# Layer 0's attention in pairs of tiles, its sums made by TensorE with the identity

## The chip, the cores and the metric

The kernel runs on one core of one Trainium2 chip. The metric is the device time of one execution in microseconds (us). The core has five engines that work side by side, each through its own queue in order: TensorE (PE in the profile; PEld is its loading of weights), VectorE (DVE), ScalarE (ACT), GpSimd (POOL) and SyncE (SP), which here only issues transfers. Products leave TensorE into PSUM, in banks of 512 float32 columns on 128 partitions; everything else lies in SBUF.

## The reference

A model of four layers, each a feed-forward half step, an attention step and the same feed-forward half step again, on `x` of shape (4, 1024, 128) in float32. What the change touches is the attention of layer 0. It is not an attention over the sequence: each token looks at its own 16 heads only.

```python
h, hd = 16, 8
Q = (x @ Wq.T).reshape(b, s, h, hd)
K = (x @ Wk.T).reshape(b, s, h, hd)
V = (x @ Wv.T).reshape(b, s, h, hd)
scores = jnp.einsum('bshd,bstd->bsht', Q, K) / math.sqrt(hd)
attn = jax.nn.softmax(scores, axis=-1)
out = jnp.einsum('bsht,bstd->bshd', attn, V).reshape(b, s, dm)
return out @ Wfc.T
```

So for each token there are 16 x 16 scores, each a sum of 8 products, and 16 x 8 outputs, each a sum of 16 products: 2048 products and 2048 again. `x` of this step is normalised (mean and variance over the 128 channels) before it goes in. The feed-forward of layer 0 is a mixture of 8 experts, of which each token uses two: a product of 128 by 512, a GELU, and one of 512 by 128. It runs before and after the attention with the same weights.

## The kernel before

**The stages.** `run` goes through the stages l0, l1_attn, l2 and l3. The residual stays in SBUF, channels on the partitions: `self.X[b]` is 128 x 1024 for each of the four batches. Stage l0 holds both expert passes of layer 0, its attention, and the first feed-forward of layer 1 (`l1_ffn`).

**The lanes.** Within stage l0 `macaron` lines up the work in lanes: one has the experts (`route` where no other lane does it, `experts`, `combine`), one the attentions (`middle0` to `middle3`) and the layer 1 feed-forwards (`last`), and a late one two of the second pass's routes. Each piece is a generator. `lanes` keeps a clock for each lane, always continues the one whose clock is behind, and adds what the generator yields: `yield 2.6` for a block of experts, `yield 11.2` for a tile of attention. A piece may name others that must be finished first: attention of batch b waits for the combination of the first expert pass of b, the second pass's route of batches 0 and 1 for `middle1`. That gives the order in which instructions are written. The framework then places instructions on the queues by its own priorities, so single instructions of both lanes interleave finely.

**An expert block** (`experts`, L424 to L474) is 128 slots of tokens for one expert: a transfer of the block's weights (L455), a gather (L457), a transpose on TensorE (L461), its copy by VectorE (L463), four products, four GELUs on ScalarE (L468), four products back, an addition on VectorE (L441) and a scatter (L442). A pass has 85 blocks: 23 for batch 0, 23 for batch 1 and 39 for batches 2 and 3 together in the first, and 39, 23 and 23 in the second. A float32 product is written once by `mm` (L227) and appears as two instructions on TensorE.

**Attention** (`l0_attn`, from L498) takes a batch in 8 tiles of 128 tokens. First the squares of the centred residual (L509) give the scale of each token (`scales`, L268 and L270). For a tile, `projected` makes queries, keys and values in one product of 384 columns, tokens on the partitions, and ScalarE scales them out of PSUM (L517). `weighed` is on VectorE: all 2048 products of queries and keys (L525), their sum over the 8 dimensions (L527), the maximum (L529), the subtraction (L530), and then ScalarE's exponential (L532). `summed`: the sum of the weights (L537), its reciprocal (L538), the 2048 products of weights and values (L542), their sum over the 16 heads (L544) and the scaling (L545). TensorE turns the tile, so that channels are on the partitions again (L562), ScalarE copies it into one of four columns of `oS` (L563), and after four tiles the product with `wfc` is added to the residual (L569). Tile i + 1 is weighed ahead of the sums of tile i. The weights of V are permuted on the host so that head comes last; those of Q and K are as given.

Of the kernel before, what the change touches and what calls it, by code (L numbers as in the profile page):

```python
# [12 lines left out]
AF = mybir.ActivationFunctionType  # L13
ALU = mybir.AluOpType
AX = mybir.AxisListType

P = 128
B, S, D = 4, 1024, 128
NH, HD = 16, 8
NE, FC = 8, 4  # L20
NT = S // P
# [87 lines left out]
def _col(v):  # L109
    return np.asarray(v).reshape(-1, 1)  # L110


def _moe_pack(w1, w2, b1, b2):

    w2 = w2.reshape(FC, P, NE, D).transpose(1, 2, 0, 3).reshape(P, NE, FC * D)
    b1 = b1.reshape(NE, FC, P).transpose(2, 0, 1)
    return np.concatenate([w1, w2, b1, np.broadcast_to(b2, (P, NE, D))], 2)


def _packs(i):  # L120

    bc = np.broadcast_to

    l0m = [
        ("w", _moe_pack(
            i["L0_ffn_w1"].transpose(2, 0, 1), i["L0_ffn_w2"].transpose(2, 0, 1), i["L0_ffn_b1"], i["L0_ffn_b2"]
        ))
    ]
    l0s = [("rw", i["L0_ffn_router_w"].T)]
    wv = i["L0_attn_Wv"].T.reshape(D, NH, HD).transpose(0, 2, 1).reshape(D, D)  # L130
    l0a = [
        ("wqkv", np.concatenate([i["L0_attn_Wq"].T, i["L0_attn_Wk"].T, wv], 1)),
        ("wfc", i["L0_attn_Wfc"].T),
    ]

    l1f = [
        ("wg", i["L1_ffn_w_gate"].T),
        ("wu", i["L1_ffn_w_up"].T),
        ("wd", i["L1_ffn_w_down"].T.reshape(HIDC, P, D).transpose(1, 0, 2)),
    ]  # L140

    w = i["L1_attn_w_qkv"]
    turned = [2 * d + 1 if d < HD // 2 else 2 * d - HD for d in range(HD)]

    heads = lambda w, order: w.reshape(P, NH, HD)[..., order].reshape(P, D)
    straight = list(range(HD))
    l1a = [
        ("wq", heads(w[:, :D], straight)),
        ("wqt", heads(w[:, :D], turned)),
        ("wk", heads(w[:, D : 2 * D], straight)),  # L150
        ("wkt", heads(w[:, D : 2 * D], turned)),
        ("wv", w[:, 2 * D :]),
        ("wo", i["L1_attn_w_out"]),
        ("bo", _col(i["L1_attn_b_out"])),
    ]

    l2m = [
        ("w", _moe_pack(
            i["L2_ffn_w1"].transpose(1, 0, 2), i["L2_ffn_w2"].transpose(1, 0, 2), i["L2_ffn_b1"], i["L2_ffn_b2"]
        ))  # L160
    ]
    l2s = [("rw", i["L2_ffn_router_w"]), ("rb", bc(i["L2_ffn_router_b"], (P, NE)))]
    l2a = [
        ("wq", i["L2_attn_Wq"].T),
        ("wkv", np.concatenate([i["L2_attn_Wk"].T, i["L2_attn_Wv"].T], 1)),
        ("bq", _col(i["L2_attn_bq"])),
        ("bk", _col(i["L2_attn_bk"])),
        ("bkv", bc(np.concatenate([i["L2_attn_bk"], i["L2_attn_bv"]]), (P, 2 * D))),
        ("gamma", bc(np.asarray(i["L2_attn_gamma"]).reshape(1, 1), (P, 1))),
    ]  # L170

    l3f = [
        ("wr", i["L3_ffn_W_r"].T),
        ("wk", i["L3_ffn_W_k"].T),
        ("wv", i["L3_ffn_W_v"].T),
        ("mur", _col(i["L3_ffn_mu_r"])),
        ("muk", _col(i["L3_ffn_mu_k"])),
    ]
    a = {k[8:]: v for k, v in i.items() if k.startswith("L3_attn_")}
    at = np.arange(P)  # L180
    turn = at % NH * HD + at // 32 + at % 32 // NH * 4
    l3a = [
        ("maa", np.concatenate([_col(a["time_maa_" + x]) for x in "xwkvrg"], 1)),
        ("w1", a["time_maa_w1"]),
        ("w2", a["time_maa_w2"][:4].reshape(P, D)),
        ("w2l", a["time_maa_w2"][4]),
        ("td", _col(a["time_decay"])),
        ("dw1", a["time_decay_w1"]),
        ("dw2", a["time_decay_w2"]),
        ("u", _col(a["time_faaaa"])),  # L190
        ("wr", a["W_r"]),
        ("wk", a["W_k"]),
        ("wv", a["W_v"][:, turn]),
        ("wg", a["W_g"][:, turn]),
        ("wo", a["W_o"][turn]),
        ("lng", _col(a["ln_gamma"][turn])),
        ("lnb", _col(a["ln_beta"][turn])),
    ]
    return {
        **_constants(),  # L200
        "l0m": l0m, "l0s": l0s, "l0a": l0a, "l1f": l1f, "l1a": l1a,
        "l2m": l2m, "l2s": l2s, "l2a": l2a, "l3f": l3f, "l3a": l3a,
    }


class Macaron:
# [291 lines left out]
    def l0_attn(self, ps, wp, m, b):  # L498
        nc = self.nc
        v = nc.vector  # L500
        X = self.X[b]
        scale = 1.0 / math.sqrt(HD)
        bank = lambda shape=(P, HALF): self.t(ps, list(shape), "bank")
        sq = self.t(wp, [P, S], "sq", bufs=1)
        for h in range(2):
            c = slice(h * HALF, (h + 1) * HALF)
            cen = bank()
            self.mm(cen, self.c0["center"], X[:, c])
            nc.scalar.activation(sq[:, c], cen, AF.Square)  # L509
        r = self.scales(ps, wp, sq, "a")  # L510
        yield 4

        def projected(i):
            pq = bank((P, 3 * D))
            self.mm(pq, X[:, i * P : (i + 1) * P], m["wqkvc"])
            qkv = self.t(wp, [P, 3, D], "qkv", bufs=3)
            nc.scalar.mul(qkv.rearrange("p a b -> p (a b)"), pq, r[:, i : i + 1])  # L517
            return qkv

        def weighed(qkv):  # L520
            q = qkv[:, 0, :].rearrange("p (h d) -> p h d", d=HD)
            k = qkv[:, 1, :].rearrange("p (t d) -> p t d", d=HD)
            sh = [P, NH, NH, HD]
            pr = self.t(wp, sh, "prod", bufs=3)
            v.tensor_tensor(pr, q.unsqueeze(2).to_broadcast(sh), k.unsqueeze(1).to_broadcast(sh), ALU.mult)  # L525
            sc = self.t(wp, [P, NH, NH], "sc")
            v.tensor_reduce(sc, pr, AX.X, ALU.add)  # L527
            mx = self.t(wp, [P, NH, 1], "mx")
            v.tensor_reduce(mx, sc, AX.X, ALU.max)  # L529
            v.tensor_tensor(sc, sc, mx.to_broadcast([P, NH, NH]), ALU.subtract)  # L530
            ex = self.t(wp, [P, NH, NH], "ex")
            nc.scalar.activation(ex, sc, AF.Exp, scale=scale)  # L532
            return ex

        def summed(qkv, ex):
            sm = self.t(wp, [P, NH, 1], "sm")
            v.tensor_reduce(sm, ex, AX.X, ALU.add)  # L537
            v.reciprocal(sm, sm)  # L538
            values = qkv[:, 2, :].rearrange("p (d t) -> p d t", d=HD)
            sh = [P, NH, HD, NH]  # L540
            pv = self.t(wp, sh, "prod", bufs=3)
            v.tensor_tensor(pv, ex.unsqueeze(2).to_broadcast(sh), values.unsqueeze(1).to_broadcast(sh), ALU.mult)  # L542
            o = self.t(wp, [P, NH, HD], "o")
            v.tensor_reduce(o, pv, AX.X, ALU.add)  # L544
            v.tensor_tensor(o, o, sm.to_broadcast([P, NH, HD]), ALU.mult)  # L545
            return o.rearrange("p h d -> p (h d)")


        qkvs = [projected(0), projected(1)]
        exs = [weighed(qkvs[0])]  # L550
        yield 6
        for i in range(NT):
            if i + 2 < NT:
                qkvs.append(projected(i + 2))
            if i + 1 < NT:
                exs.append(weighed(qkvs[i + 1]))
            k = i % 4
            if k == 0:
                oS = self.t(wp, [P, HALF], "oS")
            o = summed(qkvs[i], exs[i])  # L560
            oT = bank((P, P))
            nc.tensor.transpose(oT, o, self.c0["ident"])  # L562
            nc.scalar.copy(oS[:, k * P : (k + 1) * P], oT)  # L563
            yield 11.2
            if k == 3:
                y = bank()
                self.mm(y, m["wfc"], oS)
                c = slice((i - 3) * P, (i + 1) * P)
                v.tensor_tensor(X[:, c], X[:, c], y, ALU.add)  # L569


# [713 lines left out]
```

## Time and profile before

| | |
|---|---|
| median of 3 runs | 3297.95 us (3294.87 to 3299.5) |
| the profiled execution's own time | 3388.92 us |
| its span, first to last instruction | 3387.1 us |
| PE busy over the span | 2861.4 us, 84% |
| DVE busy | 1793.1 us, 53% |
| ACT busy | 1614.4 us, 48% |
| POOL busy | 973.6 us, 29% |
| mean granted TensorE clock | 0.888 of full speed |
| layer 0's attention, first to last instruction | about 160 to 711 us of the span |
| start of layer 1's attention | about 949 us |

Times in the prediction are from the profiled execution unless they are said to be of the timed runs. "Busy" is the time in which an engine has an instruction under way; for TensorE the ends of instructions are modelled and lengths of neighbours overlap, so a busy TensorE can still have room, and the distance between the starts of instructions tells more. "Idle before" is the engine's idle time ahead of a group of instructions and what ended it. The clock is the share of full speed that was granted to TensorE.

### The profile page before, as it was taken

The numbers are of one execution on the slowest core, as the hardware profiler recorded it, in microseconds if no ns is written. First come the engines' busy times: TensorE is split into PE (matmuls) and PEld (weight loads), VectorE is DVE, ScalarE is ACT, GpSimd is POOL, SyncE is SP. The second block draws the span as 40 slices with busy tenths as digits, with TensorE's granted clock in tenths as the row PEclk, the third lists the DMA queues.
The fourth block names the chain that finished last, engine by engine and source line by source line (L and its number), as shares of the span: only waits on it lengthen the run. The fifth ranks groups of instructions, "written<-read, shape, count | busy, mean of one in ns | idle before, by whom it ended". The sixth has DMA issues, their size and how long they took to land.

```text
span 3387.1 us, 48419 instructions
## 1 busy us (share of the span) xinstructions
PE 2861.4 (84%) x18126; PEld 1672.3 (49%) x18126; DVE 1793.1 (53%) x3048; ACT 1614.4 (48%) x3546; POOL 973.6 (29%) x972
## 2 busy tenths in 40 slices
PE   6777758778779999999999998987968877688887
PEld 6655547556533333333333335676757856223323
DVE  3387776853136776776776742434454422354353
ACT  4555525567404665665665663454423444322432
POOL 2465506433330000000000000353404444254353
PEclk7888959889879999999999998998978979687888
DMA  5565516544400000000000000475624656000000
GB/s 169 166 186 172 174 45 188 168 123 134 149 13 2 6 6 4 6 6 16 6 6 3 1 1 18 135 218 170 185 71 144 193 166 188 13 0 7 7 0 13
DMA packets 122890, 277.64 MB, mean 82 GB/s; under 512 B 18016, under 2 KB 67296, under 8 KB 122528
## 3 DMA queue, kind: packets, MB, share of 16 engines
q1 hardware_dynamic: 101792, 231.77, 23.1%
q0 software_dynamic: 20864, 42.77, 4.1%
q8 instruction: 144, 2.36, 0.3%
q14 instruction: 90, 0.74, 0.1%
HBM read 238.43 MB, written 31.85 MB: 80 GB/s over the span
## 4 chain that ended last, share of the span: by engine, by line
PE 68%; DVE 13%; POOL 5%; issue 5%; ACT 5%; DMA 4%; another core or an unknown queue 0%; SPq 0%; POOLq 0%; DVEq 0%; ACTq 0%
PE bank L227 37%; PE two L227 16%; PE o L227 8%; PE s L227 4%; DMA c_y<-res 2%; DVE nm L717 2%; POOL z L1078 1%; DMA res<-e_y,g_target 1%; DVE prod L542 1%; ACT e_h L468 1%; DVE sc L527 1%; POOL res L442 1%; DVE prod L525 1%; PE bank L461 1%; PE wave L227 1%
## 5 line engine op out<-in xcount | busy, mean ns | idle before, releaser
L717 DVE TENSOR_REDUCE nm<-two 128x2 f32<-128x1024 f32 x512 | 626.8, 1224 | 289.2 <-PE s L227 269.8
L740 ACT ACTIVATE e<-s 128x512 f32<-128x512 f32 x1024 | 555.8, 595 | 403.5 <-PE s L227 400.5
L468 ACT ACTIVATE e_h<-bank,e_w 128x128 f32<-128x128 f32 x1304 | 453.3, 367 | 544.2 <-PE bank L227 445.6
L227 PE MATMUL bank<-e_x,e_w 128*128 128x128 f32 x2608 | 573.0, 318 | 152.4 <-ACT e_h L468 61.5
L227 PE MATMUL s<-qm,kz 32*128 32x512 f32 x2048 | 633.5, 642 | 0.8 <-ACT e L740 0.8
L227 PE MATMUL two<-kz,qz 32*128 32x512 f32 x2048 | 592.1, 663 | 19.5 <-DVE nm L717 2.5
L457 POOL DMA_INDIRECT e_xg<-rows,g_source x326 | 328.5, 1008 | 942.1 <-DVE g_target L412 347.5
L227 PEld LDWEIGHTS bank<-e_x,e_w 128*128 128x128 f32 x2608 | 413.8, 203 | 290.4 <-ACT e_h L468 124.3
L442 POOL DMA_INDIRECT res<-e_y,g_target x326 | 376.1, 1154 | 319.5 <-DVE e_y L441 179.9
L227 PE MATMUL bank<-e_w,e_h 128*128 128x128 f32 x2608 | 450.7, 289 | 15.7 <-ACT e_h L468 12.9
L227 PEld LDWEIGHTS bank<-e_w,e_h 128*128 128x128 f32 x2608 | 378.4, 202 | 29.5 <-ACT e_h L468 22.3
L227 PE MATMUL o<-e,va 128*32 128x256 f32 x4096 | 328.3, 392 | 0.1
L441 DVE TENSOR_TENSOR e_y<-bank,e_w 128x128 f32<-128x128 f32 x326 | 94.4, 290 | 438.3 <-PE bank L227 379.5
L227 PEld LDWEIGHTS two<-kz,qz 32*128 32x128 f32 x2048 | 159.3, 188 | 237.5 <-issue 161.0
L227 PEld LDWEIGHTS o<-e,va 128*32 128x32 f32 x4096 | 81.0, 108 | 389.6 <-issue 370.3
L227 PEld LDWEIGHTS s<-qm,kz 32*128 32x128 f32 x2048 | 206.5, 183 | 11.4 <-issue 7.7
L705 POOL COPY va<-vd 128x256 f32<-128x256 f32 x16 | 6.7, 432 | 624.4 <-PE o L227 538.1
L463 DVE COPY e_x<-bank 128x128 f32<-128x128 f32 x326 | 92.8, 285 | 93.6 <-PE bank L461 73.2
L493 PE MATMUL bank<-c,c_y 128*128 128x128 f32 x128 | 39.5, 453 | 111.8 <-DVE c_y L490 111.8
L227 PE MATMUL bank<-g_cols,g_lanes 128*128 128x39 f32 (+1 forms) x512 | 83.3, 321 | 25.5 <-DVE g_cols L392 24.8
L1078 POOL TENSOR_TENSOR z<-st,r 128x512 f32<-128x512 f32 x64 | 96.0, 1503 | 22.7 <-DVE st L1072 22.4
L461 PE MATMUL bank<-c,e_xg 128*128 128x128 f32 x326 | 94.5, 290 | 7.6 <-DMA e_xg<-rows,g_source 7.6
(302 smaller groups left out, 3778.1 us busy)
## 6 DMA issues: line engine op xcount, KB each, us to landing
e_w<-in_l0m_dram SPq DMA_DIRECT2D x170, 578.0 KB
e_w<-in_l2m_dram SPq DMA_DIRECT2D x156, 578.0 KB
c_y<-res SPq DMA_DIRECT2D x32, 512.0 KB
rows<-g_xt SPq DMA_DIRECT2D x16, 512.0 KB
e_xg<-rows,g_source POOLq DMA_INDIRECT x326
res<-e_y,g_target POOLq DMA_INDIRECT x326
x<-in_x_dram SPq DMA_DIRECT2D x4, 512.0 KB
qz<-qd SPq DMA_DIRECT2D x64, 32.0 KB
```

The lines of the kernel that those rows point to most:

```text
L227: self.nc.tensor.matmul(out, lhsT, rhs, start=start, stop=stop)
L441: nc.vector.tensor_tensor(y, o, w[:, MOE_W - D :], ALU.add)
L442: ins = nc.gpsimd.indirect_dma_start(out=res[:, :], out_offset=at(target[:, k : k + 1]), in_=y, in_offset=None)
L457: nc.gpsimd.indirect_dma_start(out=xg, out_offset=None, in_=rows[:, :], in_offset=at(source[:, k : k + 1]))
L461: nc.tensor.transpose(tp, xg, self.c0["ident"])
L463: nc.vector.tensor_copy(x, tp)
L468: nc.scalar.activation(h[:, fc, :], up[:, fc, :], func, bias=w[:, 2 * FC * P + fc : 2 * FC * P + fc + 1])
L493: nc.tensor.transpose(tp[:, j, :], y[1][:, i, :], self.c0["ident"])
L525: v.tensor_tensor(pr, q.unsqueeze(2).to_broadcast(sh), k.unsqueeze(1).to_broadcast(sh), ALU.mult)
L717: v.tensor_reduce(nm[:, it, h, 2 * pair : 2 * pair + 2], s, AX.X, ALU.max, negate=True)
L740: nc.scalar.activation(es[g], s, AF.Exp, scale=scale)
L1078: pool.tensor_tensor(z, st[:, 0:HALF], r, ALU.mult)
```

## The change

Attention takes two tiles at a time. Queries and keys are now permuted on the host so that the dimension of a head comes first and the head last; values are no longer permuted. VectorE still makes all the products, but the sums over them are made by TensorE: the products of a pair lie in 8 planes, one for each dimension, of 2 x 256 numbers, and 8 products of the identity with a plane add up in one PSUM bank, which then holds the scores of both tiles. The maximum and the subtraction read that bank. The weights are scaled before they meet the values; the products of weights and values lie in 16 planes of 128 x 128, one for each head summed over, and 16 products with such a plane as the stationary side and the identity as the moving one add up in PSUM. These come out turned, channels on the partitions, so that the transpose is gone; one copy serves both tiles. The buffers for qkv grow from 3 to 6, those for the first products are one of both tiles instead of three of one, and the second products have two of their own. The pieces that `lanes` counts are 5 and 8 for a pair instead of 11.2 for each tile.

```diff
-    wv = i["L0_attn_Wv"].T.reshape(D, NH, HD).transpose(0, 2, 1).reshape(D, D)
+    inner = lambda w: w.T.reshape(D, NH, HD).transpose(0, 2, 1).reshape(D, D)
     l0a = [
-        ("wqkv", np.concatenate([i["L0_attn_Wq"].T, i["L0_attn_Wk"].T, wv], 1)),
+        ("wqkv", np.concatenate([inner(i["L0_attn_Wq"]), inner(i["L0_attn_Wk"]), i["L0_attn_Wv"].T], 1)),
...
-            qkv = self.t(wp, [P, 3, D], "qkv", bufs=3)
+            qkv = self.t(wp, [P, 3, D], "qkv", bufs=6)
...
-        def weighed(qkv):
-            q = qkv[:, 0, :].rearrange("p (h d) -> p h d", d=HD)
-            k = qkv[:, 1, :].rearrange("p (t d) -> p t d", d=HD)
-            sh = [P, NH, NH, HD]
-            pr = self.t(wp, sh, "prod", bufs=3)
-            v.tensor_tensor(pr, q.unsqueeze(2).to_broadcast(sh), k.unsqueeze(1).to_broadcast(sh), ALU.mult)
-            sc = self.t(wp, [P, NH, NH], "sc")
-            v.tensor_reduce(sc, pr, AX.X, ALU.add)
-            mx = self.t(wp, [P, NH, 1], "mx")
+        def multiplied(pair):
+            sc = bank((P, 2, NH, NH))
+            pr = self.t(wp, [P, 2, HD, NH, NH], "prod", bufs=1)
+            for j, qkv in enumerate(pair):
+                q, k = (qkv[:, n, :].rearrange("p (d h) -> p d h", d=HD) for n in range(2))
+                sh = [P, HD, NH, NH]
+                v.tensor_tensor(pr[:, j], q.unsqueeze(3).to_broadcast(sh), k.unsqueeze(2).to_broadcast(sh), ALU.mult)
+            for d in range(HD):
+                self.mm(sc, self.c0["ident"], pr[:, :, d], start=d == 0, stop=d == HD - 1)
+            return sc
+
+        def weighed(sc):
+            mx = self.t(wp, [P, 2, NH, 1], "mx")
             v.tensor_reduce(mx, sc, AX.X, ALU.max)
-            v.tensor_tensor(sc, sc, mx.to_broadcast([P, NH, NH]), ALU.subtract)
-            ex = self.t(wp, [P, NH, NH], "ex")
-            nc.scalar.activation(ex, sc, AF.Exp, scale=scale)
+            ex = self.t(wp, [P, 2, NH, NH], "ex")
+            v.tensor_tensor(ex, sc, mx.to_broadcast([P, 2, NH, NH]), ALU.subtract)
+            nc.scalar.activation(ex, ex, AF.Exp, scale=scale)
             return ex
 
-        def summed(qkv, ex):
-            sm = self.t(wp, [P, NH, 1], "sm")
+        def summed(pair, ex):
+            sm = self.t(wp, [P, 2, NH, 1], "sm")
             v.tensor_reduce(sm, ex, AX.X, ALU.add)
             v.reciprocal(sm, sm)
-            values = qkv[:, 2, :].rearrange("p (d t) -> p d t", d=HD)
-            sh = [P, NH, HD, NH]
-            pv = self.t(wp, sh, "prod", bufs=3)
-            v.tensor_tensor(pv, ex.unsqueeze(2).to_broadcast(sh), values.unsqueeze(1).to_broadcast(sh), ALU.mult)
-            o = self.t(wp, [P, NH, HD], "o")
-            v.tensor_reduce(o, pv, AX.X, ALU.add)
-            v.tensor_tensor(o, o, sm.to_broadcast([P, NH, HD]), ALU.mult)
-            return o.rearrange("p h d -> p (h d)")
+            v.tensor_tensor(ex, ex, sm.to_broadcast([P, 2, NH, NH]), ALU.mult)
+            oT = bank((P, 2, P))
+            for j, qkv in enumerate(pair):
+                values = qkv[:, 2, :].rearrange("p (t d) -> p t d", d=HD)
+                sh = [P, NH, NH, HD]
+                pv = self.t(wp, sh, "pv")
+                v.tensor_tensor(
+                    pv, ex[:, j].rearrange("p h t -> p t h").unsqueeze(3).to_broadcast(sh),
+                    values.unsqueeze(2).to_broadcast(sh), ALU.mult,
+                )
+                for t in range(NH):
+                    self.mm(oT[:, j], pv[:, t].rearrange("p h d -> p (h d)"), self.c0["ident"], start=t == 0, stop=t == NH - 1)
+            return oT
 
-        qkvs = [projected(0), projected(1)]
-        exs = [weighed(qkvs[0])]
+        pairs = [[projected(0), projected(1)]]
+        ex = weighed(multiplied(pairs[0]))
         yield 6
-        for i in range(NT):
...
-            o = summed(qkvs[i], exs[i])
-            oT = bank((P, P))
-            nc.tensor.transpose(oT, o, self.c0["ident"])
-            nc.scalar.copy(oS[:, k * P : (k + 1) * P], oT)
-            yield 11.2
+        pairs.append([projected(2), projected(3)])
+        for n in range(NT // 2):
+            sc = multiplied(pairs[n + 1]) if 2 * n + 2 < NT else None
+            yield 5
+            if 2 * n + 4 < NT:
+                pairs.append([projected(2 * n + 4), projected(2 * n + 5)])
+            if n % 2 == 0:
+                oS = self.t(wp, [P, HALF], "oS")
+            oT = summed(pairs[n], ex)
+            nc.scalar.copy(oS[:, n % 2 * 2 * P : (n % 2 + 1) * 2 * P], oT.rearrange("p i t -> p (i t)"))
+            if sc is not None:
+                ex = weighed(sc)
+            yield 8
```

More of the change, by code (lines that the diff above doesn't have):

```diff
@@ L545, in summed @@
-            v.tensor_tensor(o, o, sm.to_broadcast([P, NH, HD]), ALU.mult)
-            return o.rearrange("p h d -> p (h d)")
-        qkvs = [projected(0), projected(1)]
-        exs = [weighed(qkvs[0])]
-        yield 6
-        for i in range(NT):
[L553 to L558, printed above, removed]
-                oS = self.t(wp, [P, HALF], "oS")
-            o = summed(qkvs[i], exs[i])
-            oT = bank((P, P))
-            nc.tensor.transpose(oT, o, self.c0["ident"])
-            nc.scalar.copy(oS[:, k * P : (k + 1) * P], oT)
-            yield 11.2
-            if k == 3:
+            v.tensor_tensor(ex, ex, sm.to_broadcast([P, 2, NH, NH]), ALU.mult)
@@ new lines, in summed @@
+            return oT
+        pairs = [[projected(0), projected(1)]]
+        ex = weighed(multiplied(pairs[0]))
+        yield 6
+        pairs.append([projected(2), projected(3)])
[5 more added lines that the diff above has]
+            if n % 2 == 0:
+                oS = self.t(wp, [P, HALF], "oS")
+            oT = summed(pairs[n], ex)
[3 more added lines that the diff above has]
+            yield 8
+            if n % 2:
@@ L566, in l0_attn @@
                 y = bank()
                 self.mm(y, m["wfc"], oS)
-                c = slice((i - 3) * P, (i + 1) * P)
+                c = slice((n - 1) * 2 * P, (n + 1) * 2 * P)
                 v.tensor_tensor(X[:, c], X[:, c], y, ALU.add)
```

## The prediction

> **What bounds the kernel now.** I read the page's busy rows and slices first, then the windows of layer 0, then the groups of VectorE, ScalarE and TensorE between 160 and 710 us (the stretch in which layer 0's attention runs beside the experts), and last a few rows of the timeline to price a product.
>
> Windows view (columns: window, length, busy us and instructions of PE, PEld, DVE, ACT, POOL, then granted clock, DMA share, GB/s):
> ```profile
> 160.00:262.00 102.00, 72.68 (x429) 58.04 (x429) 85.10 (x114) 59.94 (x130) 60.63 (x45) 0.88 0.57 167
> 283.00:412.00 129.00, 101.04 (x649) 80.55 (x648) 97.81 (x145) 81.14 (x186) 83.11 (x64) 0.98 0.61 184
> 424.00:500.00 76.00, 38.79 (x166) 31.54 (x166) 59.37 (x97) 19.69 (x71) 0.00 (x0) 0.57 0.14 46
> 680.00:710.00 30.00, 13.79 (x55) 9.70 (x55) 26.64 (x38) 12.14 (x28) 5.40 (x5) 0.58 0.14 38
> 700.00:800.00 100.00, 91.80 (x562) 70.93 (x563) 42.22 (x120) 75.35 (x155) 40.63 (x41) 0.97 0.51 148
> ```
> While experts and attention overlap, VectorE is the fullest engine (85.10 of 102). In the third and fourth rows attention runs with a route, or almost alone, and TensorE idles with its clock down to 0.57. From 700 on attention is over and TensorE is the full one: 91.80 of 100.
>
> VectorE's and ScalarE's groups in 160 to 710 (mean ns after the busy us, then idle time before it):
> ```profile
> L525 DVE TENSOR_TENSOR prod<-qkv 128x2048 f32<-128x2048 f32 x32 | 73.0, 2285 | 0.7 <-ACT qkv L517 0.7
> L527 DVE TENSOR_REDUCE sc<-prod 128x256 f32<-128x2048 f32 x32 | 72.8, 2276 | 0.0
> L544 DVE TENSOR_REDUCE o<-prod 128x128 f32<-128x2048 f32 x32 | 72.7, 2271 | 0.0
> L542 DVE TENSOR_TENSOR prod<-ex,qkv 128x2048 f32<-128x2048 f32 x32 | 72.2, 2255 | 0.0
> ...
> L468 ACT ACT_TABLE_LOAD x31 | 39.8, 1283 | 6.7 <-issue 3.3 <-PE bank L227 2.9
> L532 ACT ACT_TABLE_LOAD x26 | 33.4, 1283 | 0.5
> ```
> Four long instructions a tile, none with idle time before it: attention never waits on anything but VectorE's queue, and the experts' two small copies (L441, L463) queue behind them.
>
> TensorE's timeline where experts run alone at full clock (start, length):
> ```profile
> 891.70 0.61 PE L227 MATMUL bank<-e_w,e_h 128*128 128x128 f32 x4
> 892.15 0.39 PE L227 MATMUL bank<-e_x,e_w 128*128 128x128 f32 x2
> 892.37 0.61 PE L227 MATMUL bank<-e_w,e_h 128*128 128x128 f32 x4
> ```
> Lengths overlap; starts tell the cost. Four instructions take 892.15 - 891.70 = 0.45 us, so 0.112 us each. One float32 product is two instructions (2608 of them in the page for 326 blocks of four products), 0.224 us. Likewise the 512-wide products of the feed-forward start 0.86 us apart (942.75, 943.61, 944.47): 0.43 per instruction.
>
> **What the Trainium skill says.** "FP8 and Floating Point Precision", TensorE Precision Notes: a true float32 product goes four times through the array. The trace agrees: 512 columns cost 0.86 us, 1.68 ns a column. "VectorE: DVE Perf Modes", the perf-mode tier table: float32 tensor_tensor and tensor_reduce run at the lowest rate, 2293 ns for 2048 elements; here 2285 and 2276. So laying the products out in planes makes none of them cheaper; only the dropped reductions save. "ScalarE: Activation LUTs", What ACT_TABLE_LOAD costs: about 1283 ns for every switch of set plus a drain; the load agrees, the drain isn't a row here. "TensorE: Matmul & The Clock Gate", What's actually happening: the array's clock halves when idle and comes back with activity; the rows above show 0.57 and 0.97.
>
> **The change, part by part, for a pair of tiles (16 pairs).**
> VectorE loses two score reductions (2 x 2.28) and two output reductions (2 x 2.27): 9.1 us. The four products stay (2 x 2.29 + 2 x 2.26 = 9.1). The small rows now take both tiles at once: before 2 x (0.408 + 0.414 + 0.411 + 0.246 + 0.285) = 3.5; after, maximum, subtraction, sum and scaling on 512 elements at about 0.69 each (L399's row, 512 elements, 0.685; its neighbours that read PSUM, L569 and L249, also 0.685 and 0.689) and a reciprocal of 0.25: 3.0. Sum: 21.7 becomes 12.1, 9.6 saved, 154 us in all. The strided read of the weights in the second product has no row; bounds 2.26 (as now) and twice that; I take 2.26, and the dearer end (2 x 2.26 x 16 = 72 us of VectorE) would still leave it far from full.
> ScalarE: 16 exponentials instead of 32, each of which now usually brings a load of its table and one back (26 + 31 loads in this stretch, 5 or so of them for square roots). About 10 to 16 pairs of loads go: 26 to 41 us of ScalarE. qkv stays; the copy of outputs is 16 of 256 columns. All this is cover, since ScalarE isn't full.
> TensorE gains 8 products of 512 columns (8 x 0.86 = 6.9) for the scores and 32 of 128 columns (32 x 0.224 = 7.2) for the turned outputs, and loses two transposes (2 x 0.112): 13.8 us a pair, 221 us in all. Weight loads ride along, as for the experts, whose every product loads its own. No DMA is added; the weights' packs keep their size.
> The order: the lanes' clock charges attention 4 + 6 + 4 x 13 = 62 a batch instead of 4 + 6 + 8 x 11.2 = 99.6, so fewer blocks (2.6 each) are put beside it: a batch now takes as long as 24 blocks. Expert lane 0 of batch 1 (23 blocks) ends with attention 0; the 39 blocks of batches 2 and 3 outlast attention 1 by 15 blocks; the second route no longer waits for attention 1. The compiler's own ordering moves single instructions too, so waits at the head of TensorE's queue are mostly filled with the other lane's products. What is late next is TensorE.
> Waits added: the 16 score instructions wait for both products of the pair (4.6 us of VectorE); behind them on TensorE stand the next block's products, and ScalarE and VectorE wait for those. The output products wait for one product each (2.26), and give VectorE the next while they run (3.6). A score bank is now held in PSUM through the previous pair's sums, one of four that the side lane shares with the routes.
>
> **The sum.** TensorE's work between 160 and 710, at full clock, from its groups there: about 2,090 instructions of 128 columns or fewer x 0.112 = 234; 64 of 384 columns x 0.32 = 20; 29 of 512 x 0.43 = 13: 267 us, 49% of 550. After: 267 + 221 = 488. It breaks even only if TensorE delivers 488 / 550 = 89% of full clock. What it delivers in this stage when it is the full engine: 700 to 800, by the same prices, has 345 + 69 instructions of 128 columns, 54 + 8 + 2 of 512 and 84 narrow ones: 414 x 0.112 + 64 x 0.43 + 84 x 0.108 = 83 us, 0.83. From 840 to 860 it is 0.90. I take 0.85: 488 / 0.85 = 574, 24 us more than 550; and 15 blocks after attention 1 run at the experts' own pace (28 us of work at about 0.74, since a block alone takes 2.56 us for 1.9 of work) instead of 0.85: 5 more. +29 us on the profiled execution's 3388.9 (span 3387.1 and 1.8 around it). The timed median is 3298, 0.973 of that: +28, **3326 us**. The rest of the kernel keeps its instructions.
>
> **Rivals.**
> *TensorE becomes the bound, a little dearer than VectorE was* (above): 3326; own range 3300 to 3365 (0.89 to 0.80 of clock).
> *TensorE swallows the sums.* For it: in 424 to 500 and 680 to 710 it is nearly idle, and these sums would fill that; the clock would stay at 1; fewer table loads and no long reductions in front of L441 and L463. At 0.95 of clock: 488 / 0.95 = 514, -36 us, -35 timed: 3263. Against: nothing before layer 1's attention shows 0.95; it decides from 0.89 up.
> *The queue's head blocks.* TensorE takes instructions in order; where the written order puts 16 score instructions ahead of a block while VectorE is late, both lanes stop. For it: TensorE waited 15.6 us for L545 at L562 already, and experts alone reach 0.74. At 0.72: 678, +128, +125 timed: 3423. Against: the full stretches above.
> *It evens out*: the 154 us taken from VectorE and the 221 put on TensorE trade one bound for another at 0.89: 3298. That the reductions stay on VectorE is excluded by the diff.
>
> **How the numbers follow.** Chances: little dearer 0.50, swallowed 0.27, blocked 0.15, even 0.08. A measurement tells about 0.2%, 6.6 us, from no change. Faster 0.28 (swallowed, a touch of even), same 0.10, slower 0.62. The range of eight in ten leaves out the far end of both tails: 3260 takes in 0.95 of clock; 3400 takes in 0.75, half of the blocked case, and the dearer strided product, which only delays TensorE's start.
>
> **What would show it.** Right: L527's and L544's rows gone, VectorE about 190 us instead of 347 in attention; two new TensorE groups, 256 instructions of 512 columns and 1024 of 128; TensorE busy over 90% from 200 to 700, the clock near 1; ScalarE's loads down by 20 or more; layer 1's attention starting at about 978 instead of 949. Wrong: the layer 0 stage ending before 940 (swallowed), TensorE's instructions waiting on VectorE's products by tens of us (blocked), or a later stage that moves.

## The result, and the profile after

The changed kernel takes 3406.73 us (median of 4 runs, 3396.01 to 3411.29) against 3298.72 us before: ratio 1.0319, interval [1.0297, 1.0341], slower by 108 us. The prediction said slower by 28, 3326 us with a range of 3260 to 3400: right in sign, a quarter of the size, and just outside the range.

One caution about the two profiles. The profiled execution of the kernel before took 3388.92 us, 3% more than its timed runs; profiled again it took 3302.8. Attention there starts at 150 us instead of 165 (by the scales of its first batch, L270), and the first products of layer 1's attention at 956.1 instead of 986.6. So below, "before" is this second profile. In the changed kernel these products start at 1058.2 us, with attention starting at 148. From the start of attention to there it is 956.1 - 150.3 = 806 us before and 1058.2 - 148.1 = 910 after: 104 us, so nearly all of the loss lies in the stage l0.

The first profile need not be a chance outlier. On the two chips of the later experiments the same kernel takes 3365 and 3387 us, and in the profiles from there attention's first products start at 162 to 172 us; in the first profile they start at 167.4, in all others at 150 to 153. So it looks like one from such a chip, but which chip it came from isn't known.

The groups of the changed kernel between 140 and 760 us, on VectorE and ScalarE:

```profile
L550 DVE TENSOR_TENSOR pv<-ex,qkv 128x2048 f32<-128x2048 f32 x32 | 73.0, 2288 | 15.3 <-PE bank L227 14.5
L527 DVE TENSOR_TENSOR prod<-qkv 128x2048 f32<-128x2048 f32 x32 | 72.4, 2282 | 1.4 <-ACT qkv L517 1.4
L534 DVE TENSOR_REDUCE mx<-bank 128x32 f32<-128x512 f32 x16 | 11.1, 691 | 78.2 <-PE bank L227 78.2
...
L468 ACT ACT_TABLE_LOAD x20 | 25.7, 1283 | 0.4
...
L537 ACT ACT_TABLE_LOAD x14 | 18.0, 1283 | 0.2
```

The reductions over 2048 elements are gone, the four products of a pair cost what they did (the strided read of the weights too: 2288 ns), a small row of both tiles costs 691 as expected, and table loads for exponentials and GELUs fell from 67 to 34. VectorE's attention rows, which hardly waited before, now wait 78.2 us for the score bank. The sums on TensorE, same stretch:

```profile
L227 PE MATMUL bank<-prod,c 128*128 128x512 f32 x256 | 129.8, 646 | 8.2 <-DVE prod L527 8.2
L227 PE MATMUL bank<-c,pv 128*128 128x128 f32 x1024 | 126.7, 275 | 0.0
```

256 and 1024 instructions, with hardly any wait in front of them: so far all as predicted. Now the stage cut at the start and end of each batch's attention (columns as in the prediction: window, length, PE, PEld, DVE, ACT, POOL, clock, DMA share, GB/s). Before, second profile:

```profile
150.00:266.00 116.00, 82.79 (x470) 65.97 (x469) 97.39 (x137) 66.32 (x151) 66.48 (x51) 0.84 0.54 162
266.00:277.00 11.00, 10.94 (x83) 9.64 (x81) 2.07 (x7) 7.58 (x18) 7.46 (x8) 1.00 0.81 274
277.00:395.00 118.00, 90.14 (x572) 71.30 (x570) 95.86 (x139) 74.23 (x170) 76.97 (x58) 0.98 0.61 188
395.00:411.00 16.00, 12.82 (x36) 8.14 (x36) 6.35 (x19) 7.25 (x19) 0.00 (x0) 0.50 0.30 84
411.00:547.00 136.00, 86.46 (x428) 72.32 (x428) 106.15 (x162) 52.04 (x147) 46.27 (x38) 0.66 0.33 105
547.00:560.00 13.00, 13.00 (x102) 11.72 (x100) 3.09 (x11) 8.94 (x21) 8.65 (x10) 1.00 0.81 270
560.00:688.00 128.00, 85.17 (x479) 68.20 (x479) 107.08 (x187) 72.30 (x174) 56.52 (x44) 0.79 0.48 143
```

After:

```profile
148.00:265.00 117.00, 111.06 (x675) 85.58 (x674) 58.37 (x79) 47.19 (x106) 51.26 (x40) 0.97 0.42 124
265.00:293.00 28.00, 15.86 (x89) 11.93 (x88) 5.52 (x17) 9.39 (x24) 5.86 (x6) 0.76 0.41 118
293.00:408.00 115.00, 109.07 (x672) 84.66 (x671) 58.19 (x78) 47.19 (x106) 51.25 (x40) 0.99 0.41 126
408.00:483.00 75.00, 60.74 (x375) 49.24 (x374) 15.83 (x56) 33.95 (x96) 29.31 (x30) 0.89 0.60 175
483.00:585.00 102.00, 94.79 (x531) 71.54 (x531) 67.34 (x104) 30.14 (x88) 18.05 (x16) 0.90 0.21 67
585.00:596.00 11.00, 11.00 (x84) 9.72 (x82) 2.76 (x9) 7.08 (x17) 6.90 (x8) 1.00 0.69 210
596.00:727.00 131.00, 121.36 (x776) 97.35 (x776) 69.08 (x129) 58.84 (x143) 56.12 (x43) 0.97 0.41 125
727.00:776.00 49.00, 33.94 (x230) 30.95 (x228) 17.95 (x75) 25.06 (x74) 17.63 (x18) 0.80 0.61 179
```

The second attention before ends with its last addition (L569) at 389, not at 395 where the window is cut. So a batch's attention takes about as long as before, or less (117, 115, 102, 131 us against 116, 112, 136, 128). But between them there are now 28, 75 and 11 us in which no attention can run, where there were 11, 22 and 12. Before, the experts' pass beside the first and the second attention had its last addition (L441) at 240 and 388, with attention running to 266 and 389; now at 271 and 456, with attention over at 265 and 408. So the pass isn't done when attention is, and the next batch's attention waits for its combination. In 408 to 483 experts run alone, their last addition at 456, and then the combination, which waits 8.9 us for its transfer; VectorE works 16 of 75 us. When the last attention is over, at 727, the pass of 39 blocks beside it runs on to 763, and the next pass turns its first block (L461) at 786; before, that pass was done at 637, some 50 us ahead of the end of attention.

Of the 104 us, 41 lie within layer 0's attention, from its first scales to its last addition (579 us against 538), and 63 behind it (331 against 268). Behind it, because fewer blocks of experts were done by then. Their second products, first before (150 to 688 us), then after (148 to 727):

```profile
L227 PE MATMUL bank<-e_w,e_h 128*128 128x128 f32 x821 | 147.9, 295 | 2.5 <-ACT e_h L468 1.1 <-DVE g_pick L328 1.1
```

```profile
L227 PE MATMUL bank<-e_w,e_h 128*128 128x128 f32 x727 | 119.5, 278 | 1.6 <-ACT e_h L468 1.5
```

At 8 instructions a block, 103 blocks are done before and 91 after. The 12 that are left over would take 31 us at the 2.57 us at which blocks follow each other alone between 412 and 456 (an estimate); the rest of the 63 us isn't split up here.

Inside a burst of attention TensorE is as full as predicted. From 293 to 408 it has 588 instructions of 128 columns or fewer, 16 of 384 and 68 of 512: 588 x 0.112 + 16 x 0.32 + 68 x 0.43 = 100 us of work in 115, 0.87. The other three bursts, counted in the same way, have 0.86, 0.82 and 0.85.

### The profile page after: what moved, and what is told of

It is laid out like the page before. It is cut to its first block, busy times and chain, and to the rows that moved or that the text cites. A ratio compares the mean times of both kernels' runs of the same rounds, so it can differ in the third digit from the quotient of the medians.

```text
span 3394.2 us, 50755 instructions
## 1 busy us (share of the span) xinstructions
PE 2998.3 (88%) x19374; PEld 1779.2 (52%) x19374; DVE 1664.2 (49%) x2904; ACT 1586.7 (47%) x3494; POOL 953.0 (28%) x972
## 4 chain that ended last, share of the span: by engine, by line
PE 73%; DVE 9%; DMA 6%; POOL 5%; issue 4%; ACT 3%; SPq 0%; POOLq 0%; DVEq 0%; ACTq 0%
PE bank L227 43%; PE two L227 16%; PE o L227 8%; PE s L227 4%; DMA c_y<-res 2%; DVE nm L727 2%; POOL z L1088 1%; DMA res<-e_y,g_target 1%; POOL res L442 1%; DMA e_w<-in_l0m_dram 1%; DMA e_w<-in_l2m_dram 1%; PE wave L227 1%; DVE st L1082 1%; PE bank L461 1%; DVE den L922 1%
## 5 line engine op out<-in xcount | busy, mean ns | idle before, releaser
L457 POOL DMA_INDIRECT e_xg<-rows,g_source x326 | 339.9, 1043 | 992.9 <-DVE g_target L412 447.0
L227 PE MATMUL bank<-e_x,e_w 128*128 128x128 f32 x2608 | 545.0, 305 | 58.6 <-DVE e_x L463 23.5
L227 PEld LDWEIGHTS bank<-e_x,e_w 128*128 128x128 f32 x2608 | 396.9, 193 | 180.8 <-DVE e_x L463 59.5
L227 PE MATMUL bank<-e_w,e_h 128*128 128x128 f32 x2608 | 426.6, 279 | 4.4 <-ACT e_h L468 4.3
L442 POOL DMA_INDIRECT res<-e_y,g_target x326 | 343.9, 1055 | 300.1 <-DVE e_y L441 194.3
L227 PEld LDWEIGHTS bank<-e_w,e_h 128*128 128x128 f32 x2608 | 357.8, 194 | 11.5 <-ACT e_h L468 9.0
L441 DVE TENSOR_TENSOR e_y<-bank,e_w 128x128 f32<-128x128 f32 x326 | 94.5, 291 | 455.8 <-PE bank L227 448.7
L227 PE MATMUL bank<-prod,c 128*128 128x512 f32 x256 | 129.8, 646 | 8.2 <-DVE prod L527 8.2
L227 PE MATMUL bank<-c,pv 128*128 128x128 f32 x1024 | 126.7, 275 | 0.0
L227 PEld LDWEIGHTS bank<-c,pv 128*128 128x128 f32 x1024 | 120.7, 192 | 1.9 <-issue 0.9
```

The lines of the kernel that those rows point to most:

```text
L227: self.nc.tensor.matmul(out, lhsT, rhs, start=start, stop=stop)
L441: nc.vector.tensor_tensor(y, o, w[:, MOE_W - D :], ALU.add)
L442: ins = nc.gpsimd.indirect_dma_start(out=res[:, :], out_offset=at(target[:, k : k + 1]), in_=y, in_offset=None)
L457: nc.gpsimd.indirect_dma_start(out=xg, out_offset=None, in_=rows[:, :], in_offset=at(source[:, k : k + 1]))
```

## The experiments

All ratios are to the kernel before on the same chip. Absolute times are compared only within the first two sets of runs, where the kernel before stood at 3298 us; in the last two it stood at 3365 and 3387. "Charge" is what a pair adds to the lanes' clock, 5 + 8 = 13 in the changed kernel; two tiles had 2 x 11.2 = 22.4 before.

**The kernel before, profiled once more.**

> The kernel before, once more, for a second profile. Its first profiled execution took 3389 us against a median of 3298. If that was an odd execution, this one is near 3298, layer 1's attention starts its products 30 to 50 us earlier than the 986.6 of the first profile, and layer 2 is shorter too.

3302.8 us; products of layer 1's attention from 956.1, 30.5 earlier. So the first profile doesn't stand for the timed runs.

**Only the score sums on TensorE.** `summed` keeps the changed kernel's pairs, and the outputs go back to VectorE:

```diff
-                for t in range(NH):
-                    self.mm(oT[:, j], pv[:, t].rearrange("p h d -> p (h d)"), self.c0["ident"], start=t == 0, stop=t == NH - 1)
+                o = self.t(wp, [P, NH, HD], "o")
+                v.tensor_reduce(o, pv, AX.X, ALU.add)
+                v.tensor_tensor(o, o, sm[:, j].to_broadcast([P, NH, HD]), ALU.mult)
+                nc.tensor.transpose(oT[:, j], o.rearrange("p h d -> p (h d)"), self.c0["ident"])
```

> The changed kernel, but only the score sums go to TensorE; the outputs are summed by VectorE and turned by two transposes a pair, as before. TensorE's extra work is 16 x 6.9 = 110 us instead of 221, VectorE keeps 73 us of reductions. The lanes' charge stays 13 a pair. Saturation (TensorE is full at about 0.86 while attention runs, so the extra work is paid in full): (267 + 110) / 547 = 0.69 of clock, below saturation, so most of the loss goes: 3270 to 3320. Wrong spread (13 a pair puts too few blocks beside attention, the rest run alone): little changes, 3360 to 3400. Coarser pieces (pairs, the score bank held in PSUM): 3380 or more.

3359.67 us, 1.0179 [1.0146, 1.0213]. Half of TensorE's extra work gone took 47 of 108 us, not most of it: between saturation and wrong spread, and not what a kernel far below saturation should do.

**The charge alone.**

```diff
-            yield 5
+            yield 10
...
-            yield 8
+            yield 14
```

> The changed kernel with the lanes' charge of a pair raised from 5 + 8 to 10 + 14, so that 9 blocks instead of 5 are written beside each pair, as before the change; the arithmetic is the same. Saturation: TensorE's work is the same and it is full while the lanes run together, so the time moves by less than 40 us from 3407: 3370 to 3420. Wrong spread: the two stretches in which only experts run (28 and 75 us long in the profile of the changed kernel) are filled, 3320 to 3350.

3335.74 us, 1.0103 [1.0066, 1.0140]. Two numbers that no engine ever sees take 71 of the 108 us, as "wrong spread" had it. Its windows, cut in the same way:

```profile
150.00:283.00 133.00, 125.31 (x782) 99.78 (x782) 65.13 (x100) 56.71 (x138) 60.26 (x52) 0.96 0.46 145
283.00:295.00 12.00, 12.00 (x87) 10.46 (x86) 3.13 (x10) 7.61 (x19) 7.44 (x8) 1.00 0.79 265
295.00:431.00 136.00, 131.64 (x877) 109.50 (x875) 63.78 (x100) 61.10 (x151) 71.49 (x57) 0.99 0.48 154
431.00:452.00 21.00, 15.38 (x63) 10.69 (x63) 7.02 (x21) 8.25 (x24) 0.00 (x0) 0.66 0.35 96
```

The pauses of 28 and 75 us are 12 and 21, as before the change. The bursts are longer, 133 and 136 instead of 117 and 115, because more blocks of experts run in them. Attention as a whole did not become shorter: its last addition is at 754 us instead of 727. The gain is what the experts have done by then (150 to 755 us):

```profile
L227 PE MATMUL bank<-e_w,e_h 128*128 128x128 f32 x913 | 151.4, 280 | 1.6 <-ACT e_h L468 1.5
```

That is 114 blocks, where the changed kernel had done 91 at the end of its attention and 97 by 755. From the last addition to layer 1's first products (989.2) it is then 235 us instead of 331.

**One pass on TensorE.** Planes and identity in float32r, which the trace lists as fp32r. The Trainium skill ("FP8 and Floating Point Precision", TensorE Precision Notes) speaks of a float32 that is read and truncated, beside the true one of four passes. That float32r is this one isn't shown by a run; what the trace shows is one instruction for each product instead of two.

```diff
-            pr = self.t(wp, [P, 2, HD, NH, NH], "prod", bufs=1)
+            pr = self.t(wp, [P, 2, HD, NH, NH], "prod", mybir.dt.float32r, bufs=1)
...
-                pv = self.t(wp, sh, "pv")
+                pv = self.t(wp, sh, "pv", mybir.dt.float32r)
```

> The changed kernel with both planes and the identity in float32r[...]. If that takes one pass instead of four, the extra work on TensorE falls from 221 to about 55 us, with the order, the pairs, the waits and the charge the same. Saturation: 267 + 55 = 322 of 547, 0.59 of clock, and VectorE 154 us lighter: below the kernel before, 3230 to 3280. Wrong spread: 3330 to 3380, since the handover gaps stay. Coarser pieces: 3380 or more. If the passes stay as they are: 3407.

3330.66 us, 1.0090 [1.0057, 1.0124]: the value of wrong spread, not of saturation. The extra work on TensorE fell to 89 us at full clock, not to 55 (worked out in the last section); (267 + 89) / 547 = 0.65 is still below saturation, and yet the kernel is 33 us above the one before.

**Pairs, with all sums on VectorE**, charged 22.4:

> Pairs of tiles in the changed kernel's loop, but all sums by VectorE as before (both reductions, two transposes a pair), the charge 9.4 + 13 a pair as two tiles had. No work is added to TensorE. It tells what pairing alone is worth: fewer small instructions (about 0.5 us a pair) and 16 exponentials instead of 32, each with up to two table loads. Saturation: 3275 to 3300, at or a little below the kernel before. Coarser pieces: well above it, 3350 or more.

3294.60 us, 0.9993 [0.9977, 1.0009]. Pairing costs nothing and, in spite of fewer table loads (43 for exponentials and GELUs instead of 67), gains nothing. The coarser pieces are excluded as a cause; that the score bank is held in PSUM isn't part of this run.

**The same, charged 13.** If the charge is a cause by itself, it must hurt a kernel whose TensorE has nothing to add up.

```diff
-            yield 9.4
+            yield 5
...
-            yield 13
+            yield 8
```

> Pairs with all sums on VectorE, but charged 5 + 8 as in the changed kernel. TensorE gets no work. If the low charge is a cause by itself (attention is written too densely, the experts beside it starve and finish alone): 40 to 90 us above the 3294.6 of the same kernel charged 22.4, so 3335 to 3385. If only a full TensorE makes it matter: 3290 to 3310.

3388.50 us, 1.0267 [1.0239, 1.0295]: 94 us above the same kernel charged 22.4. Its windows show such pauses too, 28 and 61 us, with VectorE the fullest engine in the burst:

```profile
249.00:277.00 28.00, 16.61 (x93) 12.58 (x93) 5.89 (x18) 10.04 (x26) 6.84 (x7) 0.76 0.45 139
277.00:390.00 113.00, 81.37 (x432) 64.63 (x431) 92.26 (x106) 53.17 (x122) 60.24 (x48) 0.82 0.46 148
390.00:451.00 61.00, 49.02 (x279) 37.96 (x279) 13.48 (x48) 27.28 (x76) 22.39 (x23) 0.82 0.57 177
```

By the end of its attention, at 707 us, 91 blocks are done, as in the changed kernel; charged 22.4 it was 105, at 679. So neither the sums on TensorE nor the planes are needed for the loss. This run and the charge alone carry the account.

**Both cures at once, and the scores with the higher charge.**

> Both at once: planes and identity in float32r (one pass instead of four[...]) and the charge of a pair raised to 10 + 14. If the load on TensorE and the low charge are two separate causes, the two gains against the changed kernel (76 and 71 us) add up: about 3260, below the kernel before. If they are one and the same (a saturated TensorE makes the experts run late, and either cure is enough): 3320 to 3335, no better than one of them.

3276.21 us, 0.9939 [0.9914, 0.9963]. The two causes are separate: 76 and 71 us would add up to 3260, and 131 of the 147 came. This version beats the kernel before by 0.6%, at the price of float32r, whose loss of precision no run here measured.

> Only the score sums on TensorE, full float32, with the charge 10 + 14. Separate causes: it takes the gain of the charge (71) on top of the first experiment's 47: about 3290, level with the kernel before. One and the same: 3335 to 3350.

3296.07 us, 0.9989 [0.9975, 1.0002]: level with the kernel before, in full float32, with half of the sums on TensorE.

So the charge has now been changed from 13 to 22.4 or 24 in four kernels, with nothing else changed: it took 71 us with both sums on TensorE, 64 with the scores alone, 94 with none, and 54 in float32r. And at the charge of 13 the scores on TensorE (1.0179) are better than no sums there (1.0267, another chip): by itself this half of the change did no harm at either charge.

**TensorE's work, priced by itself.** Scores added up twice, `scale` halved:

```diff
-            for d in range(HD):
-                self.mm(sc, self.c0["ident"], pr[:, :, d], start=d == 0, stop=d == HD - 1)
+            for d in range(2 * HD):
+                self.mm(sc, self.c0["ident"], pr[:, :, d % HD], start=d == 0, stop=d == 2 * HD - 1)
```

> The changed kernel charged 10 + 14, with every score product added up twice (the exponential's scale is halved, so the computation is the same). It prices TensorE's work by itself: 16 x 6.9 = 110 us more, no other work, the same charge. Saturation: TensorE delivers about 0.86 of clock while the lanes overlap, so the 110 us cost 110 to 130: 3445 to 3465. If TensorE still has room there: under 3400.

1.0403 [1.0362, 1.0443]. Against 1.0103 and 1.0148 for the two measurements of the same kernel without the second sum (three chips in all), that is 2.6 to 3.0%, 84 to 99 us of 3298 for 110 us of work at full clock: less than the 110 to 130 expected, and far from nothing. Once TensorE is full, its work is paid for nearly in full. Some of this can be the longer wait for the score bank, which the run doesn't set apart.

**How high a charge.**

> The changed kernel charged 14 + 20 for a pair instead of 5 + 8. If more blocks beside attention go on helping: 3300 to 3320. If 24 has already closed the gaps and what is left is TensorE's work: 3325 to 3360.

> The changed kernel charged 8 + 11 = 19. If the best charge is the one at which attention lasts as long as the expert pass beside it (23 blocks x 2.6 = 60 of the lanes' clock for 4 pairs and 10 more would be 12.5; the 39 blocks, 101, would be 23): between the 1.032 of 13 and the 1.010 of 24, nearer to the second, 1.012 to 1.02.

34 gives 1.0234 [1.0186, 1.0281], 19 gives 1.0184 [1.0152, 1.0215]. With 1.0319 at 13 and 1.0103 or 1.0148 at 24, 24 is the best of the four; more charge isn't always better. On the scale of 3298, 34 is 3375: both branches of its expectation lay below that, and why it is worse than 24 stays open.

> Planes and identity in float32r, charged 8 + 11. A pair now costs VectorE 12 us and TensorE about 4, so its best charge may be lower than 24. If what matters is that attention lasts as long as the experts beside it: 3280 to 3310, between the 3331 of 13 and the 3276 of 24. If the right charge is a pair's own cost: below 3276.

1.0068 [1.0051, 1.0084]: in one pass too, 19 is between 13 (1.0090) and 24 (0.9939), and nearer to the first; on the scale of 3298 it is 3320, above both branches of the expectation. The best charge is not a pair's own cost, which is much lower here.

**Scores or outputs.** Only the outputs on TensorE, scores reduced by VectorE:

> Only the outputs are summed and turned by TensorE, in full float32; scores stay on VectorE; charged 10 + 14. Extra work on TensorE 16 x 7.0 = 112 us. If the price of a sum on TensorE is its time there: level with the kernel that moves only the scores, 3285 to 3310. If the turned outputs are cheaper than that (no wait for a transpose, one copy for two tiles): under 3285.

1.0099 [1.0060, 1.0138], 3331 on the scale of 3298: above both branches, and the whole of the rest, where the scores alone had cost nothing. These two stood on different chips, so they were measured again side by side:

> The changed kernel charged 10 + 14, measured beside the next three on one chip. Ratio to the kernel before as measured: 1.010.

> Only the score sums on TensorE, charged 10 + 14. If a sum's price is its time on TensorE, scores and outputs (110 and 112 us) cost the same, and both have about half of the loss: 1.005 here and in the next. If scores are free and outputs are not: 0.999 as measured.

> Only the outputs on TensorE, charged 10 + 14. Same price as the scores: 1.005. Outputs dearer: 1.010 as measured on the other chip.

Both 1.0148 [1.0117, 1.0180], scores 1.0006 [0.9993, 1.0020], outputs 1.0108 [1.0074, 1.0142]. It holds: the first 110 us on TensorE are free when they are the scores, and cost about 1.1% when they are the outputs. Part of it shows in the waits of TensorE from 150 to 800 us. First the kernel with outputs only, then the one with scores only (engine and line waiting, releaser, us in total, times, longest):

```profile
PE bank L227 <- DVE pv L549: 29.6, 5, 13.9
```

```profile
PE bank L227 <- DVE prod L527: 14.9, 8, 5.1
```

In the first, output products stand at the head of TensorE's queue up to 13.9 us before VectorE has made their planes. But in the kernel with both sums no such wait for pv appears, and it isn't cheaper. Why outputs cost more than scores stays open. Two rivals weren't run: all three kernels stand at one charge, which may suit the scores better, and they don't have the same number of buffers for their products.

## Why the prediction was right or wrong

**The operations were priced right.** VectorE's rows, the strided product, the small rows of a pair, the numbers of instructions on TensorE and their cost: all within a few per cent. Table loads fell by 33, where I had 20 to 32. That ScalarE's and pairing's savings are only cover is shown by pairs on VectorE: 0.9993.

**TensorE becoming the bound was right, but the term was too small.** I took 0.85 of full clock; the bursts show 0.82 to 0.87. This term was 24 us of the sum; with the charge at 24 the kernel stands 1.0103 above the one before, and 1.0148 on another chip, 34 to 49 us of 3298. The price of work past that point, 84 to 99 us for 110, agrees. Not foreseen: within it, the scores are free and the outputs aren't.

**The step that failed is the order.** The prediction worked the lanes' clock through (62 a batch instead of 99.6, attention 1 over with 15 blocks to go) and then priced it at 5 us, as a difference of pace: those blocks at 0.74 of clock instead of 0.85. It should have asked what attention does meanwhile. It can't run: the next batch's attention waits for the combination behind those blocks, and the experts alone use VectorE for 16 of 75 us. Before, attention was written long enough to last until the pass beside it was done (266 against 240 us, 389 against 388). And the blocks that were not done beside attention, 12 of them, came on top at its end, which the prediction left out too. The term put at 5 us measured 71 us in the changed kernel and 94 in the kernel with all sums on VectorE.

Behind it is one wrong assumption: 0.85 was a share measured where TensorE is the full engine, and was applied to the whole of 160 to 710 us. From 148 to 727 us there are 2840 narrow instructions, 64 of 384 columns and 284 of 512, 461 us of work in 579: 0.80, with 0.82 to 0.87 in the bursts and 0.41 and 0.59 in the two pauses.

**The rivals.** "TensorE swallows the sums" holds for the scores alone (0.9989 and 1.0006) and for one pass (0.9939), not for the whole. "The queue's head blocks" was wrong as a cause: in the changed kernel TensorE waits 8.2 us for VectorE's products in all. It had the right size, 3423, for a mechanism that wasn't there. The range cut this size off at 3400. The signs to look for included the lateness of layer 1's attention: 978 predicted, and by the same mark, the zeroing of its buffers on GpSimd, 1020.6 measured (its products come later, at 1058). But none of them watched the pauses between attentions.

**The base.** The sum was made against an execution 3% longer than the timed runs, and scaled by 0.973. In the second profile the stretch is 538 us (150 to 688) and not 550, with 264 us of work and not 267, and the saturation term becomes (264 + 221) / 0.85 - 538 = 33 instead of 24. That is near the 34 us left at the charge of 24 on one chip and well under the 49 on the other.

**A reading.** That VectorE is the fullest engine while the lanes overlap holds for the first window of the prediction; in the second, TensorE has 101.04 us busy against 97.81. By the starts of its instructions TensorE does only 78 us of work in those 129, 0.60, so the argument stands, but the row quoted doesn't show it.

## What to carry to other kernels

Where two pieces of work run side by side in an order made from estimates, a change of an operation is also a change of the order: look first at what each lane can do when the other isn't done, and price the pauses, and what is left over when one lane is done, not only the pace. Shares of an engine hold for the stretch they were read in; ask for every stretch which work may run there at all. And test a restructured stage with the old charges before judging the operations: here two constants held two thirds of the loss, or half by the measurement on another chip (1.0148 of 1.0319).

## What the runs showed of the hardware

In float32r, at full clock, a product of 512 columns is one instruction of about 0.24 us (eight in 2.10 us, of which the last is 0.39 long, at 289 us of the kernel with both cures) instead of two of 0.43, 3.5 times cheaper. Where the granted clock was 0.50 (443 to 448 in the same trace), eight took 3.75 us, and the last seven start 0.43 us apart. One of 128 columns is also one instruction instead of two, but still 0.114 us (twelve in 1.53, at 180), so it costs half of what it did: the extra work was 16 x (8 x 0.24 + 32 x 0.114) = 89 us, not the 55 expected. So the narrow products don't fall to a fourth of the time. That each of these loads its own weights is one reading; it wasn't tested. How many passes a product takes no trace shows, neither here nor in the prediction's 0.86 us.

The second product reads its weights with a stride of 16 values (L550) and takes 2288 ns, about as much as the one without (2255, L542 in the prediction).
